# Moving the loads and stores of a second Strassen level to two other DMA queues, and two activations to later places

## The chip, the cores and the metric

The kernel runs on one core of one Trainium2 chip. A core has five engines with an instruction queue each: TensorE (PE: matrix products into the banks of PSUM, with its weight loads PEld beside them), VectorE (DVE), ScalarE (ACT), GpSimd (POOL) and SyncE (SP). [...] SyncE, ScalarE and GpSimd can issue DMA transfers, which 16 DMA engines carry out; the issue is an instruction in the queue of the engine that makes it, and what stands behind it in that queue comes after it. The metric is the device time of one execution in microseconds (us).

## What is computed

A layer: normalization, attention over the feature axis, residual; normalization, gated feed-forward, residual. Its weights gate, up and down are looked up by index in a table of 16 floats.

```python
def _L0_ffn_ref(x, lut, gate_idx, up_idx, down_idx):
    def _ghost_linear(x, idx, lut):
        w = lut[idx]
        return jnp.einsum('bsh,oh->bso', x, w)
    gate = _ghost_linear(x, gate_idx, lut)
    up = _ghost_linear(x, up_idx, lut)
    h = jax.nn.silu(gate) * up
    return _ghost_linear(h, down_idx, lut)
x = x + _L0_attn_ref(_layernorm(x, axis=-1), Wq, Wk, Wv, Wo)
x = x + _L0_ffn_ref(_layernorm(x, axis=-1), lut, gate_idx, up_idx, down_idx)
```

x is (2, 2048, 512) in fp32, so 4096 rows of 512 features; the inner width is 1376; all is fp32. The change lies in gate, up and their product h.

## The kernel before, in words

The 4096 rows are 8 chunks of 512, taken in 4 pairs p = 0 to 3. The inner width is 11 tiles f = 0 to 10, of 128 columns and a last one of 96. One **unit** (f, p) computes h for 128 inner columns and two chunks: h0 for chunk 2p, h1 for chunk 2p + 1. It takes gate and up together as one 2 x 2 block product and does it in Strassen's way (Winograd's form), with seven products instead of eight. A product of a unit is two matmuls of 128x128 by 128x512; each matmul shows as two records in the profile. Their sums pass through the banks a (two), b, c (two): product a1 goes into bank a, ScalarE copies it out to p1, a2 is added into the same bank, ScalarE copies u2, a3 is added, VectorE takes c22, a4 is added, and so on. **TensorE may add the next product into the bank only when the copy before has been made**: a2 waits for the copy p1 (L1058), a3 for the copy u2 (L1082).

For f = 2 to 9 there is a **second level**: some of a unit's products belong to a further 2 x 2 block product over two tiles f (even, odd) and two pairs p (even, odd), of which there are three, c, b and d (class Second, L888), with the banks z, x and w, one each. A unit then has a role: 0 is (even f, even p), 1 is (even, odd), 2 is (odd, even), 3 is (odd, odd); the tiles f = 0, 1 and 10 have none. The group of four units is spread over time, since all p of an even f come first, so parts of the sums have to be kept:

- Second.sums (L897): during units (1, 2) to (2, 0) VectorE makes the operand sums T1, T2, T4 for each of c, b, d and the two groups g of pairs, 18 tiles of 256 KB in four rotating buffers "rt". Each is stored to DRAM, far_c0T1 and so on (L908).
- Second.load (L917): loads() asks for them again ahead of a unit: six (T2 and T1 of the three) for the unit after a role-0 unit's start, that is ahead of (even f, even p) for (even f, odd p), and three (T4) ahead of (even f, last p) and (odd f, second p) for the role-2 unit that follows (L920).
- Second.part (L952): in role 1 six sums (r6 and r5 of c, d, b) are copied out of their banks by ScalarE into an "rt" buffer and stored to DRAM (L963); in role 2 r5 is added to by an accumulating DMA on GpSimd's queue (L958).
- Second.add_part (L965): in roles 2 and 3 a kept part of b is added to p1, one of c to v, by accumulating loads on GpSimd's queue (L968).
- Second.back (L970): in roles 2 and 3 a kept part of d is loaded into y (L973), which has one buffer. Role 2 adds w's product to y, and a4 adds y to bank a to give h1.

Line.run (L1190) writes the order out by hand: the steps of a unit u, with those of the unit before it, `last`, between them. Each call of between() puts work of VectorE into the gap: sums that are due, or a slice of the lookup of the next weights. The order is that of each engine's instructions, except on GpSimd, whose queue is ordered by a scheduler. In words, a unit is: a1 and the copy of bank a (p1); gap; for roles 1 to 3 of `last` the product h0 with u2 and h0's store; extra0 (z); c1 with the copies p7 and, in roles 2 and 3, v; gap; extra1; `last`'s a4 with the sum and silu of h1; a2 and the copy u2 (for role 3 a2 comes before `last`'s a4); gap; extra2; c2; `last`'s product of h1 with c22 and h1's store (end); gap; extra3; then b (h0's sum and silu) and a3 (c22), in this order for role 0, role 2 and units without a role, with a gap between and after.

The temporaries p1 (roles 1 to 3), p7, u2, v, y, c22, h0 and h1 have one buffer each, so the next unit's copy waits for the last reader. The index tiles of the lookup (two buffers) are loaded on GpSimd's queue (L311, L330, L359).

In the diff, file lines from L1146 on move by a few: L1156 of the kernel before (h0's product) is L1159 after, L1146 (h0's silu) is L1144 or, for role 1, L1149, L1178 (h1's silu) is L1184, L1181 (h1's product) is L1187, L1138 and L1165, L1170 (copies h0, h1) are L1135, L1168, L1173.

Of the kernel before, what the change touches and what calls it, by code (L numbers as in the profile page):

```python
# [55 lines left out]
AF = mybir.ActivationFunctionType  # L56
# [13 lines left out]
def tile_attn_ffn(  # L70
# [13 lines left out]
    nc = tc.nc  # L84
# [51 lines left out]
    def sub(dest, a, b):  # L136
        nc.vector.tensor_tensor(dest, a, b, ALU.subtract)

    def add(dest, a, b):
        nc.vector.tensor_tensor(dest, a, b, ALU.add)  # L140
# [337 lines left out]
    def left(t, name, order=("S2", "S4", "S1")):  # L478
        a11, a21 = t[:, 0:2, :H], t[:, 0:2, H:]
        a12, a22 = t[:, 2:4, :H], t[:, 2:4, H:]  # L480

        def s3():
            for tag in order:
                o.new(tag)
            sub(a21, a11, a21)
            o.update({"11": a11, "12": a12, "22": a22, "S3": a21})

        o = Operand(name, [
            s3, lambda: sub(o["S2"], a22, a21), lambda: sub(o["S4"], a12, o["S2"]),
            lambda: add(o["S1"], o["S2"], a11),  # L490
        ])
        return o
# [111 lines left out]
    class Square:  # L604
# [7 lines left out]
        def mm(self, ps, a, b, first):  # L612
            for m in range(2):
                for k in range(2):

                    nc.tensor.matmul(
                        ps[:, m, :], self.a[a][:, k, m * P : (m + 1) * P], self.b[b][:, k, :],
                        start=first and m == k == 0, stop=k == 1,
                        skip_group_check=not (first and m == 0),
                    )  # L620
# [50 lines left out]
    class Softmax:  # L671
# [20 lines left out]
        def end(self, h):  # L692
            r = slice(2 * h, 2 * h + 2)
            nc.vector.reciprocal(self.inv[:, r], self.sum[:, r])
            for m in range(2 * h, 2 * h + 2):
                nc.scalar.activation(
                    self.a[:, m, :], self.a[:, m, :], AF.Copy, scale=self.inv[:, m : m + 1]
                )

    gram_out(1)  # L700
    g = [g_ops[0], left(gs[1], "g_1")]
# [186 lines left out]
    class Second:  # L888
# [8 lines left out]
        def sums(self, g):  # L897

            (b11, b21), (b12, b22) = (self.operand(2 * g + h) for h in range(2))
            r = self.right[g] = {"11": b11, "21": b21, "22": b22, "T3": b12}  # L900

            def made(tag, u, v):
                r[tag] = x2p.tile([P, CH], F32, tag="rt", name=f"{tag}_{self.name}{g}", bufs=RT)
                sub(r[tag], u(), v())
                far = self.far[g, tag] = dram.tile(
                    [P, CH], F32, tag=f"{self.name}{g}{tag}", name=f"far_{self.name}{g}{tag}"
                )
                nc.sync.dma_start(far, r[tag])  # L908

            return [  # L910
                lambda: made("T1", lambda: b12, lambda: b11),
                lambda: made("T2", lambda: b22, lambda: r["T1"]),
                lambda: sub(b12, b22, b12),
                lambda: made("T4", lambda: b21, lambda: r["T2"]),
            ]

        def load(self, g, *tags):  # L917
            for tag in tags:
                t = x2p.tile([P, CH], F32, tag="tt", name=f"{tag}_{self.name}{g}_in", bufs=9)
                nc.sync.dma_start(t, self.far[g, tag])  # L920
                self.right[g][tag] = t

        def ready(self, f):
# [28 lines left out]
        def part(self, u, tag, onto=False):  # L952

            g = u.p // 2
            t = x2p.tile([P, CH], F32, tag="rt", name=f"{tag}_{self.name}_{u.name}", bufs=RT)
            nc.scalar.copy(t, self.ps)
            if onto:
                nc.gpsimd.dma_start(self.parts[g, tag], t, accum_op=ALU.add)  # L958
                return
            to = self.parts[g, tag] = dram.tile(  # L960
                [P, CH], F32, tag=f"{self.name}{g}{tag}", name=f"part_{tag}_{self.name}_{u.name}"
            )
            nc.sync.dma_start(to, t)  # L963

        def add_part(self, u, dest):  # L965
            tag = {2: "r6", 3: "r5"}.get(u.role)
# [3 lines left out]
        def back(self, u):  # L970

            t = u.temp("y")
            nc.sync.dma_start(t, self.parts[u.p // 2, {2: "r6", 3: "r5"}[u.role]])  # L973
            return t

    RT = 4
# [6 lines left out]
    of_d = Second("d", "w", lambda f: in_two(gu[f]["S4"]), lambda p: in_two(xs[p]["22"]))  # L983
# [42 lines left out]
    class GateUp:  # L1026
# [52 lines left out]
        def a2(self):  # L1079
            mm(self.a, self.pairs("S2", "T2"), False)  # L1080
            self.u2 = self.temp("u2")
            nc.scalar.copy(self.u2, self.a)  # L1082
            if self.role == 2:
                self.y = of_d.back(self)

        def c2(self):
            if self.role is None:
# [30 lines left out]
        def extra3(self):  # L1118
            if self.role == 1:
                of_d.go_on(self, "S1", "T1")  # L1120
                of_d.part(self, "r5")
                of_b.go_on(self, "S1", "T1")
                of_b.part(self, "r5")
            elif self.role == 2:
                of_d.begin(self, "S3", "T3")
                of_d.part(self, "r5", onto=True)
                add(self.y, of_d.ps, self.y)
            elif self.role == 3:
                self.y = of_d.back(self)

        def b(self):
            self.h0 = h0 = self.temp("h0")
            if self.role is None:
                mm(self.p1, self.pairs("12", "21"), False)
            elif self.role == 0:  # L1135
                of_b.begin(self, "11", "11")
                mm(self.p1, of_b.pair(self, "12", "21"), False)
                nc.scalar.copy(h0, of_b.ps)  # L1138
                add(h0, self.p1, h0)
            elif self.role == 1:  # L1140
                of_b.go_on(self, "S4", "22")
                add(h0, of_b.ps, self.p1)
            elif self.role == 2:
                of_b.go_on(self, "22", "T4")  # L1144
                add(h0, of_b.ps, self.p1)
            nc.scalar.activation(h0, self.p1 if self.role in (None, 3) else h0, AF.Silu)  # L1146

        def a3(self):
            mm(self.a, self.pairs("S1", "T1"), False)  # L1149
# [9 lines left out]
        def a4(self):  # L1159
            self.h1 = h1 = self.temp("h1")  # L1160
            if self.role is None:
                mm(self.a, self.pairs("S4", "22"), False)
            elif self.role == 0:
                of_d.begin(self, "11", "11")
                nc.scalar.copy(h1, of_d.ps)  # L1165
                mm(self.a, of_d.pair(self, "12", "21"), False)
                add(h1, self.a, h1)
            elif self.role == 1:  # L1168
                of_d.go_on(self, "S4", "22")
                nc.scalar.copy(h1, of_d.ps)  # L1170
                add(h1, self.a, h1)
            else:
                if self.role == 2:  # L1173
                    mm(self.a, of_d.pair(self, "22", "T4"), False)
                add(h1, self.a, self.y)
            if self.p == NPR - 1:
                ended[0] = self.f + 1
            nc.scalar.activation(h1, self.a if self.role is None else h1, AF.Silu)  # L1178

        def end(self):  # L1180
            nc.vector.tensor_tensor(self.h1, self.h1, self.c22, ALU.mult)  # L1181
            self.store(self.h1, 2 * self.p + 1)

    class Line:  # L1184
# [5 lines left out]
        def run(self, u, final=False):  # L1190
            last, self.last = self.last, u

            def last_a4():
                if last is not None:
                    last.a4()
                    self.between()

            role = getattr(u, "role", None)
            u.a1()
            self.between()  # L1200
            if getattr(last, "role", None):
                last.first()
            u.extra0()
            u.c1()
            self.between()
            u.extra1()
            if role != 3:
                last_a4()
            u.a2()
            self.between()  # L1210
            if role == 3:
                last_a4()
            u.extra2()
            u.c2()
            if last is not None:
                last.end()
            self.between()
            u.extra3()
            one, two = (u.a3, u.b) if final or role in (1, 3) else (u.b, u.a3)
            one()  # L1220
            self.between()
            two()
            if not role:
                u.first()
            self.between()

        def flush(self):
            self.last.a4()
            self.last.end()
            self.last = None  # L1230

    pace = [1.0]
# [94 lines left out]
    class Down:  # L1327
# [96 lines left out]
        def first(self):  # L1424
            pass

        extra0 = extra1 = extra2 = extra3 = first

        def end(self):
            pass  # L1430

    rows_in, normed_in = {}, []

# [22 lines left out]
    for (f, p), following in zip(units, units[1:] + [(NFT, 0)]):  # L1456
# [24 lines left out]
        u = GateUp(f, p)  # L1481
# [16 lines left out]
    for (part, c), following in zip(parts, parts[1:] + [None]):  # L1498
        nxt = None
        for jj in range(2):  # L1500
# [18 lines left out]
            u = units.pop(0)  # L1519
# [64 lines left out]
```

## Time and profile before

| | |
|---|---|
| median of 3 runs | 1088.44 us (1086.99 to 1089.98) |
| the profiled execution | 1091.63 us, of which its span 1089.8 us |
| TensorE busy | 1070.0 us, 98% of the span |
| VectorE busy | 838.6 us, 77% |
| ScalarE busy | 399.5 us, 37% |
| GpSimd busy | 85.7 us, 8% |
| granted TensorE clock, mean of the span | 0.994 |
| DMA moved | 189.06 MB, 173 GB/s |
| gate-and-up stage | from about 298 us to 818 us of the span |

Busy time counts instructions that compute; an engine that waits or issues a DMA is not busy. TensorE's busy time takes a matmul's modelled end, so 98% says that there is hardly a gap between matmuls, not that they run at their peak. The span is the time from the first to the last instruction; the rest of the execution's time lies around it. "a <- b" in a wait reads: a could start when b had ended. Names are without buffer numbers, so `h` is h0 or h1, `y<-part_r_d` is the load of y, `T_c_in<-far_c1T` one of Second.load's. In a row of the timeline the square brackets hold the engine's idle time before the instruction and what ended it.

### The profile page before, as it was taken

To read this page: it belongs to the slowest core of one execution; us is meant where nothing else is said; L and a number is where in the kernel's file an instruction comes from. 1 tells how busy PE (TensorE), PEld (TensorE's weight loads), DVE (VectorE), ACT (ScalarE), POOL (GpSimd) and SP (SyncE) were. 2 spreads that over 40 slices of the span, in tenths; PEclk is the share of its full clock that TensorE was granted. 3 is DMA by queue.
4 is the path that set the end of the run, shared out by engine and by line. 5 is a ranking of instruction groups with operands and counts; after the bars stand their busy time and mean duration, and the time that the engine had idled before them with its cause. 6 is when DMAs were issued, how large, how long until landed. Compare 5 with 4: busy or idle time off the path is not lost. (4 is left out here: it accounts for less than half of the span.)

```text
span 1089.8 us, 11426 instructions
## 1 busy us (share of the span) xinstructions
PE 1070.0 (98%) x3410; PEld 639.8 (59%) x3410; DVE 838.6 (77%) x1838; ACT 399.5 (37%) x759; POOL 85.7 (8%) x126
## 2 busy tenths in 40 slices
PE   9999999999999989999999998999999999999998
PEld 5668886444444434434444443444348888888887
DVE  7888777889885979789689988865629999555554
ACT  4652522554622224434444443444323322211111
POOL 0000000021110000220121022013000000000000
PEclk9999999999999989999999999999999999999999
DMA  8750314588651365785495588559526675656773
GB/s 345 224 164 20 77 40 97 138 231 217 172 140 39 144 203 202 187 184 205 147 223 175 193 198 186 190 171 199 146 73 217 203 236 173 209 177 222 226 227 117
DMA packets 127070, 189.06 MB, mean 173 GB/s; under 512 B 18576, under 2 KB 54672, under 8 KB 126112
## 3 DMA queue, kind: packets, MB, share of 16 engines
q1 hardware_dynamic: 93888, 140.55, 39.9%
q0 software_dynamic: 13056, 31.01, 14.7%
q10 hardware_dynamic: 20064, 16.78, 4.8%
q8 instruction: 27, 0.44, 0.2%
q14 instruction: 35, 0.29, 0.1%
HBM read 108.60 MB, written 79.69 MB: 173 GB/s over the span
## 5 line engine op out<-in xcount | busy, mean ns | idle before, releaser
L779 PE MATMUL y<-m,nT 128*128 128x512 f32 x256 | 110.2, 592 | 0.0
L1021 PE MATMUL c_g<-xb,wu 128*128 128x512 f32 (+1 forms) x176 | 84.4, 603 | 0.0
L779 PEld LDWEIGHTS y<-m,nT 128*128 128x128 f32 x256 | 48.6, 190 | 60.4 <-issue 57.4
L1021 PE MATMUL a_g<-xb,wg 128*128 128x512 f32 (+1 forms) x176 | 83.7, 598 | 0.0
L1021 PE MATMUL a_g<-xT_a,s 128*128 128x512 f32 (+1 forms) x176 | 83.2, 595 | 0.5 <-ACT p L1058 0.3
L1021 PE MATMUL a_d<-dT,hs_a 128*128 128x256 f32 x288 | 72.6, 379 | 0.0
L463 PE MATMUL gp<-xn_a 128*128 128x128 f32 (+3 forms) x256 | 70.1, 434 | 1.1 <-DVE xn_a L181 0.8
L1021 PE MATMUL a_g<-xT_sq,s 128*128 128x512 f32 (+1 forms) x132 | 63.2, 601 | 3.1 <-ACT u L1082 3.1
L463 PEld LDWEIGHTS gp<-xn_a 128*128 128x128 f32 x256 | 43.9, 190 | 28.0 <-issue 15.1
L1021 PEld LDWEIGHTS c_g<-xb,wu 128*128 128x128 f32 (+1 forms) x176 | 33.6, 191 | 43.6 <-issue 43.4
L1021 PEld LDWEIGHTS a_g<-xb,wg 128*128 128x128 f32 (+1 forms) x176 | 33.4, 190 | 43.9 <-issue 39.8
L1021 PEld LDWEIGHTS a_d<-dT,hs_a 128*128 128x128 f32 x288 | 54.5, 189 | 7.7
L1021 PEld LDWEIGHTS a_g<-xT_a,s 128*128 128x128 f32 (+1 forms) x176 | 32.6, 187 | 44.4 <-issue 39.2
L294 DVE COPY_PREDICATED wd<-b_wd,wd 128x512 f32<-128x512 int16 (+1 forms) x77 | 56.4, 732 | 1.3
L1387 ACT COPY p_d<-a_d 128x256 f32<-128x256 f32 x32 | 11.9, 372 | 120.8 <-PE a_d L1021 120.8
L140 DVE TENSOR_TENSOR r<-r,p_d 128x256 f32<-128x256 f32 x64 | 27.0, 421 | 27.0 <-ACT p_d L1387 17.0
L282 DVE TENSOR_SCALAR wd<-idx_wd,lut_x,lut_sb 128x512 int32<-128x512 int32 (+1 forms) x88 | 46.0, 538 | 0.7 <-DMA hd<-h 0.7
L1021 PEld LDWEIGHTS a_g<-xT_sq,s 128*128 128x128 f32 (+1 forms) x132 | 24.7, 189 | 36.4 <-issue 28.8
L140 DVE TENSOR_TENSOR u<-c_g,u 128x512 f32<-128x512 f32 (+1 forms) x28 | 19.3, 688 | 34.5 <-PE c_g L1021 31.9
L140 DVE TENSOR_TENSOR c<-a_g,p 128x512 f32<-128x512 f32 (+1 forms) x44 | 30.1, 685 | 17.5 <-PE a_g L1021 17.1
L140 DVE TENSOR_TENSOR r<-r,a_d 128x256 f32<-128x256 f32 x64 | 26.6, 416 | 22.0 <-PE a_d L1021 21.9
L1146 ACT ACTIVATE h<-h 128x512 f32<-128x512 f32 x24 | 15.1, 631 | 76.5 <-DVE h L140 69.5
(342 smaller groups left out, 2206.3 us busy)
## 6 DMA issues: line engine op xcount, KB each, us to landing
hd<-h SPq DMA_DIRECT2D x80, 256.0 KB, 2.2
h<-hd SPq DMA_DIRECT2D x40, 512.0 KB, 6.2
nl<-nd SPq DMA_DIRECT2D x32, 256.0 KB, 5.8
xnd<-xn_f ACTq DMA_DIRECT2D x16, 512.0 KB, 6.1
fl<-xnd POOLq DMA_DIRECT2D x32, 256.0 KB, 6.7
xn_back<-xnd SPq DMA_DIRECT2D x32, 256.0 KB, 4.4
rd<-r SPq DMA_DIRECT2D x32, 256.0 KB, 3.1
r<-rd SPq DMA_DIRECT2D x32, 256.0 KB, 3.6
```

The source lines that it names most:

```text
L140: nc.vector.tensor_tensor(dest, a, b, ALU.add)
L282: vec.tensor_scalar(dest.bitcast(I32), idx, lut_x[:rows, k : k + 1], lut_i[:rows, at : at + 1], ALU.bitwise_and, ALU.bitwise_xor,)
L294: vec.copy_predicated(dest, masks[level - 1], t)
L463: nc.tensor.matmul(gp[b][i][:, i * P :], xn[:, i, j % 2, :], xn[:, i:, j % 2, :], start=c % CPB == 0 and j == 0, stop=c % CPB == CPB - 1 a ...
L779: nc.tensor.matmul(ys[k], nTs[k][:, i, :], m[:, i, :], start=(i == 0), stop=(i == KB - 1))
L1021: nc.tensor.matmul(ps, lhsT, rhs, start=first and i == 0, stop=i == len(pairs) - 1, skip_group_check=not first,)
L1146: nc.scalar.activation(h0, self.p1 if self.role in (None, 3) else h0, AF.Silu)
L1387: nc.scalar.copy(p1, self.a)
```

## The change

It gives four kinds of DMA another queue, and moves four steps:

- Second.sums stores the operand sums from GpSimd's queue, not SyncE's (18 transfers of 256 KB).
- Second.load loads them on ScalarE's queue (72), and Second.part stores role 1's parts there (48).
- Second.back loads y on GpSimd's queue (16). In role 2 it is called in extra3, where it was called behind a2, and w's product is added to y in a4, one unit later, where it was added in extra3.
- Role 1's silu of h0 is called behind the next unit's a1, so behind its copy of bank a, where it stood at the end of b.
- The silu of h1 is called in end (behind c2), where it stood in a4; the product of h1 with c22 and the store move to a new step, out, behind extra3.

SyncE's queue keeps the stores of h0 and h1 in this stage. The products and sums themselves, and TensorE's order, stay.

```diff
@@ Second.sums
-                nc.sync.dma_start(far, r[tag])
+                nc.gpsimd.dma_start(far, r[tag])
@@ Second.load
-                nc.sync.dma_start(t, self.far[g, tag])
+                nc.scalar.dma_start(t, self.far[g, tag])
@@ Second.part
-            nc.sync.dma_start(to, t)
+            nc.scalar.dma_start(to, t)
@@ Second.back
-            nc.sync.dma_start(t, self.parts[u.p // 2, {2: "r6", 3: "r5"}[u.role]])
+            nc.gpsimd.dma_start(t, self.parts[u.p // 2, {2: "r6", 3: "r5"}[u.role]])
@@ GateUp.a2
             nc.scalar.copy(self.u2, self.a)
-            if self.role == 2:
-                self.y = of_d.back(self)
@@ GateUp.extra3
             elif self.role == 2:
                 of_d.begin(self, "S3", "T3")
                 of_d.part(self, "r5", onto=True)
-                add(self.y, of_d.ps, self.y)
-            elif self.role == 3:
+            if self.role in (2, 3):
                 self.y = of_d.back(self)
@@ GateUp.b
-            nc.scalar.activation(h0, self.p1 if self.role in (None, 3) else h0, AF.Silu)
+            if self.role != 1:
+                nc.scalar.activation(h0, self.p1 if self.role in (None, 3) else h0, AF.Silu)
+
+        def silu(self):
+
+            if self.role == 1:
+                nc.scalar.activation(self.h0, self.h0, AF.Silu)
@@ GateUp.a4
                 if self.role == 2:
                     mm(self.a, of_d.pair(self, "22", "T4"), False)
+                    add(self.y, of_d.ps, self.y)
                 add(h1, self.a, self.y)
             if self.p == NPR - 1:
                 ended[0] = self.f + 1
-            nc.scalar.activation(h1, self.a if self.role is None else h1, AF.Silu)
 
         def end(self):
+            nc.scalar.activation(self.h1, self.a if self.role is None else self.h1, AF.Silu)
+
+        def out(self):
             nc.vector.tensor_tensor(self.h1, self.h1, self.c22, ALU.mult)
             self.store(self.h1, 2 * self.p + 1)
@@ Line.run
             u.a1()
+            if last is not None:
+                last.silu()
             self.between()
...
             u.extra3()
+            if last is not None:
+                last.out()
             one, two = (u.a3, u.b) if final or role in (1, 3) else (u.b, u.a3)
@@ Line.flush
             self.last.end()
+            self.last.out()
```

Class Down, which the same line runs afterwards, gets the new steps as empty ones.

More of the change, by code (lines that the diff above doesn't have):

```diff
@@ L1425, in first @@
             pass
-        extra0 = extra1 = extra2 = extra3 = first
-        def end(self):
-            pass
+        extra0 = extra1 = extra2 = extra3 = silu = end = out = first
     rows_in, normed_in = {}, []
```

## The prediction

> **What bounds the kernel now.** I read the page first (TensorE busy 98% of the span), then TensorE's waits, which say where it stands still, and then the timeline around each of them. The waits (waiting instruction, who released it, total us, times, longest):
>
> ```profile
> PE z_g L1021 <- DVE lc L137: 5.3, 1, 5.3
> PE a_g L1021 <- ACT p L1058: 4.8, 4, 1.9
> PE a_g L1021 <- ACT u L1082: 3.1, 2, 1.9
> ```
>
> All of them fall into the gate-and-up stage, between 399 and 674 us. Elsewhere TensorE runs matmul behind matmul, 0.43 us a record (`PE a_g L1021 x8` takes 3.43 us in the chain), so the change can gain only what these stalls cost. The timeline (start, duration, what, idle before it and its releaser) shows the worst of the second and third kind, units (7,2) and (7,3):
>
> ```profile
> 659.01 0.68 DVE L140 TENSOR_TENSOR h<-a_g,y 128x512 f32<-128x512 f32 x1
> 659.72 0.32 SPq L973 DMA_DIRECT2D y<-part_r_d  x1
> ...
> 666.37 0.69 DVE L140 TENSOR_TENSOR y<-w_g,y 128x512 f32<-128x512 f32 x1 [2.59 <-DMA y<-part_r_d]
> 666.98 0.68 DVE L140 TENSOR_TENSOR h<-x_g,p 128x512 f32<-128x512 f32 x1
> ...
> 667.69 0.63 ACT L1146 ACTIVATE h<-h 128x512 f32<-128x512 f32 x1 [5.86 <-DVE h L140]
> ...
> 668.23 0.57 ACT L1058 COPY p<-a_g 128x512 f32<-128x512 f32 x1
> ...
> 668.85 1.98 PE L1021 MATMUL a_g<-xT_x,s 128*128 128x512 f32 x4 [1.75 <-ACT p L1058]
> ...
> 672.07 0.59 ACT L1076 COPY v<-c_g 128x512 f32<-128x512 f32 x1 [2.05 <-DVE u L140]
> ...
> 672.92 0.59 ACT L1082 COPY u<-a_g 128x512 f32<-128x512 f32 x1 [0.26 <-DVE h L1156]
> ...
> 673.56 2.86 PE L1021 MATMUL a_g<-xT_sq,s 128*128 128x512 f32 x4 [1.87 <-ACT u L1082]
> ```
>
> y has one buffer, so its load starts when the last y has been added (659.7) and lands 6.6 us later. VectorE needs it at once for y += w and stands 2.59 us. Behind that in its queue stands h0's sum, behind that ScalarE's silu, behind that in ScalarE's queue the copy of bank a (p), on which TensorE waits. The same delay comes again through v and u2. After a stall the clock is lower too (granted clock 0.83 in 670 to 680 us): the next eight records take 2.65 and 2.58 us a four instead of 1.72. The same happens at 476.65 (VectorE 2.69 us) and 570.67 (1.72 us).
>
> The first kind comes at the last operand sums of f = 1:
>
> ```profile
> 385.28 2.38 SPq L908 DMA_DIRECT2D far_c1T<-T_c  x3
> ...
> 392.77 0.69 DVE L137 TENSOR_TENSOR T_b<-xb,T_b 128x512 f32<-128x512 f32 x1 [5.86 <-DMA far_c1T<-T_c]
> ...
> 399.50 2.08 PE L1021 MATMUL z_g<-T_c_in,lc 128*128 128x512 f32 x2 [5.32 <-DVE lc L137]
> ```
>
> The store far_c1T1 stands on SyncE's queue behind six T loads (382.18 to 385.1 us) and lands after 7.4 us. Its "rt" buffer (4) is wanted again at 386.9, so VectorE stands 5.86 us and the sums lc come late.
>
> **What the stalls cost.** Start to start, against 0.43 us a record. First y place: c starts 475.39, the u2 product should start ten records later, at 479.69, and starts at 483.51: 3.8 us. Second: 577.26 instead of 574.67: 2.6. Third: 673.56 instead of 669.52, and 1.8 more on the slow clock: 5.8. Sum 12.2. The far stall: z at 399.50 instead of 394.03, then 5.29 us for the next six records instead of 2.58: 8.2.
>
> **y.** Loading y moves to GpSimd's queue (16 DMAs), role 2's add from the gap behind w's product to the next unit's a4, about ten program matmuls (8.6 us) later. The load still waits for the same buffer (h's add, 659.7), so it is not sooner. GpSimd is then in the store part_r_b (until 660.2). An accumulating load of that queue takes 0.87 us to issue and a median of 4.7 us to land (3.8 to 7.2), so y is there at 665 to 667.5, and is wanted at about 670: the stall is gone with 2 us to spare. Without that cover it would be late by what the landing exceeds. What is late next: VectorE gains the wait and 0.6 us of the add, so u2 += v comes 3.3, 2.3 and 3.2 us sooner at the three places. Followed through v's and u2's copies (0.59 us each) TensorE then waits 0.2, 0.4 and 1.0 us at the u2 product.
>
> **ScalarE's issues.** It gets 48 part stores and 72 T loads. It has issued such DMAs before only in the first stage, with four pieces to a row:
>
> ```profile
> 30.95 0.80 ACT L236 ACTIVATE n<-x,nmr_a,rstd_a 128x512 f32<-128x512 f32 x1
> 31.77 0.58 ACTq L562 DMA_DIRECT2D nd<-n  x1
> 32.40 0.81 ACT L236 ACTIVATE xn_a<-x,nmr_a,rstd_a 128x512 f32<-128x512 f32 x1 [0.66 <-ACT n L236]
> ...
> 488.16 0.38 SPq L920 DMA_DIRECT2D T_b_in<-far_b0T  x1
> ...
> 488.64 0.38 SPq L920 DMA_DIRECT2D T_d_in<-far_d0T  x1
> ```
>
> An issue there is 0.52 us; SyncE's same shape (xn_back) starts at 0.52, and its part stores and T loads are 0.32 to 0.41. I take the lower bound, since engine and shape agree: 0.5 us for a store with its gap, 0.47 for a load (488.16 to 488.64). Upper bound 1.1 us, the longest T loads on SyncE (1.09, 1.22).
> - Role 1, eight units: in the burst at 410 us the copies r_d, r_b, h1's silu (now here), a cast, r_d, r_b and their stores end at 414.93 instead of 414.2; the product on x wants it at 415.13. I take 0.15 us a unit: 1.2 us (0 to 2.8, with 0.52 for an issue).
> - Six loads ahead of the copy of bank a, 2.8 us. Into (f,2): loads end near 418.3, the copy was 418.11, TensorE wants it by 420.28: nothing. Into units (4,0), (6,0), (8,0): the silu of h0 waits for the store of the last h0 to land (675.93 at the third place) or for p's accumulation; 3.2 us sooner at the third, it ends at 672.6, loads to 675.4, copy to 676; TensorE wants it at 674.67, nine and a half us after a1. So 1.3, 1.1 and 1.5 us at the three places, the stalls above included: 3.9 (0 to 7.8, if p lands late). It takes the place of 12.2: gain 8.3.
> - Three loads into (f,1) and slow issues at a full DMA (1.22 us at 642.6): I take 1.0 us (0 to 3).
>
> **far by GpSimd's queue (18 stores), T loads by ScalarE's.** The loads can go after silu of h0 at 379.4, 2.8 us sooner, and the store no longer stands behind them. It is made at 383.76, lands after 4.7 to 7.2 us as GpSimd's others do: 388.5 to 391 instead of 392.77. VectorE gains 1.8 to 4.3 us; I take 3.0. TensorE then stands 2.5 us, and I leave 1.5 us for the slow clock: 4.2 us gained (0 to 7). In the earlier sums (362 us) VectorE may lose 1 to 2 us, hidden by its idle 1.49 us at 377.13.
>
> **The moved silus.** The same 0.63 us each; role 1's goes behind the copy of bank a, h1's behind u2's copy. ScalarE waits 34.8 us for h1's sum and 69.5 us for h0's, but only the stalls above reach TensorE: nothing beyond them. If the later store of h1 held the next h1 copy, ScalarE would stand; it has 6.9 us for product, store and landing (0.7 + 0.3 + 2.1).
>
> **Sum.** -8.3 - 4.2 + 1.2 + 1.0 = -10.3 us. The profiled execution (span 1089.8 us, 1091.6 with what lies around it) would come to a span of 1079.5; it ran 3.2 us above the median of three, 1088.44, so the median comes to 1078.1.
>
> **Rivals.** (1) ScalarE's queue becomes the bound, slower. At 1.1 us an issue a burst of six takes 6.6 us, 3.8 more: 3 x 3.8 into (4,0), (6,0), (8,0); 4 x 2.4 into (f,2), where 1.4 us is free; 1.5 into (2,0): 22.5 us, net +12.2, 1100.6 us. It decides from 0.85 us an issue. For it: SyncE's T loads did reach 0.83 to 1.22 when the DMA engines were full, and a blocked issue holds ScalarE's copies, not idle SyncE; so does an issue whose semaphore (the program shares eight among SyncE's and ScalarE's transfers) is still taken by a transfer under way. Against it: their median is 0.38 to 0.41.
> (2) The far store gains nothing: six loads of 256 KB before it move 1.6 MB whichever queue asks, and the engines' share is 0.8 to 1.0 in such stretches. Then -10.3 + 4.2: 1082.3 us. [...] The trace can't settle it: here one queue carried both.
> (3) VectorE's backlog keeps the stalls: it is busy 0.9 in 440 to 470 and 660 to 690, and the y add only moves. Only the 0.6 us of the add, through p and u2, is won at each place: 3.6; no far gain; 2.4 lost: 1087.2. Against it: the waits of 1.7 to 2.7 us are idle time, and the whole delay of silu follows them.
>
> **How the numbers follow.** Forecast 0.48, (1) 0.22, (2) 0.17, (3) 0.13. The likeliest's own range is 1072 to 1085, from the bounds of its terms; the range is 1070 to 1094, which leaves out most of the worst of (1). A change below 0.3% (3.3 us, 1085.2 to 1091.7) could not be told from none. Faster: forecast and (2), 0.65; same: (3), less what of it is faster, 0.12; slower: 0.23.
>
> **What would show it.** Right: no VectorE wait on y before h0's sum; TensorE's waits on p and u2 below 1.6 us each at 477, 572, 667; a wait on b (L1058) at the start of (4,0), (6,0), (8,0) of about 1 us, with six T loads on ScalarE's queue before it; VectorE's far wait at 387 below 4.1 us. Wrong: T loads on ScalarE's queue over 0.85 us apart, ScalarE behind TensorE at every (f,2), or VectorE standing as long on far as before.

## The result and the profile after

| | before | after |
|---|---|---|
| median | 1087.8 us (4 runs, 1086.99 to 1089.98) | 1078.45 us (4 runs, 1077.27 to 1080.96) |
| ratio, 95% interval | | 0.9914 (0.989 to 0.9938) |
| the profiled execution | 1091.63 us, span 1089.8 | 1077.27 us, span 1075.3 |
| TensorE's waits in the gate-and-up stage | 13.2 us | 5.8 us |
| mean granted clock | 0.994 | 1.000 |

The change saves 9.4 us by the medians, but 14.4 us between the two profiled executions: that of before lies at the upper end of what the kernel before took in later runs (most of them between 1085 and 1091 us), that of after is the shortest of its four. What follows from the two traces is the places, not the total.

TensorE's waits of the changed kernel in that stage (who waited, for whom, total us, times, longest), and after them the only wait of VectorE's there for a far store:

```profile
PE a_g L1021 <- ACT b_g L1058: 4.3, 3, 2.0
PE z_g L1021 <- DVE lc L137: 1.2, 1, 1.2
PE z_g L1021 <- ACT r_c L956: 0.3, 1, 0.3
```

```profile
DVE T_b L137 <- DMA far_c1T<-T_c: 1.8, 1, 1.8
```

The waits on p and u are gone, the wait on lc has shrunk from 5.3 to 1.2 us, and three waits for a copy of bank a are new. VectorE waits for y nowhere. The timeline at units (7,2) and (7,3), where the worst y stall of before lay:

```profile
648.67 1.15 POOL L973 DMA_DIRECT2D y<-part_r_d  x1
...
652.38 0.68 DVE L140 TENSOR_TENSOR h<-x_g,p 128x512 f32<-128x512 f32 x1
653.10 0.63 ACT L1144 ACTIVATE h<-h 128x512 f32<-128x512 f32 x1 [2.11 <-DVE h L140]
...
654.70 0.59 ACT L1058 COPY p<-a_g 128x512 f32<-128x512 f32 x1 [0.97 <-PE a_g L1021]
...
658.64 0.67 DVE L140 TENSOR_TENSOR y<-w_g,y 128x512 f32<-128x512 f32 x1
```

y is still asked for only when its buffer comes free, but its sum now stands behind h0's sum in VectorE's queue, ten microseconds after the load. So h0's sum, its silu and the copy p no longer wait for that DMA; ScalarE waits for TensorE (0.97 us), no longer TensorE for ScalarE.

The start of the same matmul in both profiles shows where the time went (lead: before minus after):

| matmul | before | after | lead, us |
|---|---|---|---|
| first on lc (z) | 399.50 | 395.67 | 3.83 |
| six records later | 404.79 | 398.35 | 6.44 |
| second z, unit (2,3) | 431.44 | 425.43 | 6.01 |
| behind (3,3)'s y stall | 483.51 | 473.69 | 9.82 |
| a2 of (4,0) | 488.66 | 479.92 | 8.74 |
| behind (5,3)'s y stall | 577.26 | 565.94 | 11.32 |
| a2 of (6,0) | 582.51 | 572.76 | 9.75 |
| behind (7,3)'s y stall | 678.79 | 662.36 | 16.43 |
| a2 of (8,0) | 680.51 | 666.24 | 14.27 |

Won: 6.4 us at f = 1, and 3.8, 2.6 and 6.7 us at the three y stalls (0.8 of the last already at 647 to 650 us, the rest at the stall itself). Lost: 0.4 us at (2,3), and 1.1, 1.6 and 2.2 us at the starts of (4,0), (6,0), (8,0). The last of these in the timeline of after:

```profile
662.70 0.63 ACT L1144 ACTIVATE h<-p 128x512 f32<-128x512 f32 x1 [1.94 <-DMA hd<-h]
662.73 0.83 ACTq L920 DMA_DIRECT2D T_c_in<-far_c0T  x2
663.59 0.54 ACTq L920 DMA_DIRECT2D T_d_in<-far_d0T  x1
664.16 0.45 ACTq L920 DMA_DIRECT2D T_b_in<-far_b0T  x1
664.64 0.45 ACTq L920 DMA_DIRECT2D T_d_in<-far_d0T  x1
665.13 0.45 ACTq L920 DMA_DIRECT2D T_b_in<-far_b0T  x1
665.62 0.57 ACT L1058 COPY b_g<-a_g 128x512 f32<-128x512 f32 x1 [2.29 <-DMA T_c_in<-far_c0T]
...
666.24 1.98 PE L1021 MATMUL a_g<-xT_sq,s 128*128 128x512 f32 x4 [2.00 <-ACT b_g L1058]
```

Six issues fill ScalarE's queue from 662.73 to 665.6; the copy that TensorE wants at 664.24 (2.00 us before its matmul starts) stands behind them.

### The profile page after: what moved, and what is told of

Read it like the earlier page. It is cut to its first block, busy times and chain, and to the rows that moved or that the text cites. A ratio compares the mean times of both kernels' runs of the same rounds, so it can differ in the third digit from the quotient of the medians.

```text
span 1075.3 us, 11377 instructions
## 1 busy us (share of the span) xinstructions
PE 1063.2 (99%) x3410; PEld 637.7 (59%) x3410; DVE 839.2 (78%) x1838; ACT 397.9 (37%) x759; POOL 104.3 (10%) x160
## 5 line engine op out<-in xcount | busy, mean ns | idle before, releaser
L1082 ACT COPY u<-a_g 128x512 f32<-128x512 f32 (+1 forms) x44 | 25.8, 586 | 66.6 <-PE a_g L1021 62.9
```

## The experiments

"Ratio" is always to runs of the kernel before on the same chip, with its 95% interval. "Half clock" is a stretch in which the profile shows a granted TensorE clock of 0.50; in this stage such a stretch lasted 3.4 or 6.8 us in the runs that had one (in the kernel before 6.8, 3.4 and 3.4 us, from 398.0, 480.0 and 674.5 us on), and half of its length is counted as its price.

### One part of the change at a time, on the kernel before

**The step of y alone.**

```diff
-            nc.sync.dma_start(t, self.parts[u.p // 2, ...
+            nc.gpsimd.dma_start(t, self.parts[u.p // 2, ...
@@ GateUp.a2, extra3
-            if self.role == 2:
-                self.y = of_d.back(self)
...
-                add(self.y, of_d.ps, self.y)
-            elif self.role == 3:
+            if self.role in (2, 3):
                 self.y = of_d.back(self)
@@ GateUp.a4
                     mm(self.a, of_d.pair(self, "22", "T4"), False)
+                    add(self.y, of_d.ps, self.y)
```

> The kernel before with the step of y alone (load of y by GpSimd's queue in extra3, w's product added in a4); loads, parts and silus stay. Forecast's theory: VectorE's three waits on y ahead of h0's sum (2.69, 1.72, 2.59 us) go, and with them 12 to 13 us of TensorE's lost time near 475, 570 and 670 us; since the T loads stay on SyncE's queue, nothing holds the copy of bank a into (4,0), (6,0), (8,0), so no more than 1.6 us comes back: 1087.8 - 11 = 1077 us, ratio about 0.990. Rival (VectorE's backlog keeps the stalls): only the 0.6 us of the add is won at each place, 3.6 us: 1084 us, ratio 0.997, and TensorE still waits over 1 us for p or u at the three places.

Measured: 1079.28 us, ratio 0.9922 (0.9909 to 0.9936). No wait of VectorE's on y ahead of h0's sum, and of TensorE's waits at the three places 0.3, 0.3 and 0.4 us for u are left, none for a copy into (4,0), (6,0), (8,0). VectorE's backlog as the cause (rival 3) is out.

**Of this step, the moved sum alone**: y stays on SyncE's queue, in its old place.

```diff
-                add(self.y, of_d.ps, self.y)
             elif self.role == 3:
@@ GateUp.a4
                     mm(self.a, of_d.pair(self, "22", "T4"), False)
+                    add(self.y, of_d.ps, self.y)
```

> The kernel before with w's product added to y in a4, one unit later, and nothing else: y's load stays on SyncE's queue where it was. Theory (the sum is made 8.6 us later, that is the whole of it): no wait on y at the three places, 1079.3 us as with the whole step of y, ratio 0.992. Rival (SyncE's queue, in which h stores and T loads stand behind the load that waits for its buffer, makes y late too): waits of 1 us or more on y or on T tiles remain, 1083 us or more, ratio 0.996.

Measured: 1078.24 us, ratio 0.9909 (0.9896 to 0.9922), the same as the whole change. Its waits, TensorE's and (last) VectorE's:

```profile
PE z_g L1021 <- DVE lc L137: 3.7, 1, 3.7
PE a_g L1021 <- ACT u L1082: 1.1, 3, 0.5
```

```profile
DVE T_b L137 <- DMA far_c1T<-T_c: 4.2, 1, 4.2
```

The far stall is still there, as nothing at f = 1 was changed; the y stalls are gone. GpSimd's queue is not needed for them.

**The far stores alone, and the T loads alone.**

```diff
-                nc.sync.dma_start(far, r[tag])
+                nc.gpsimd.dma_start(far, r[tag])
```

> The kernel before with the far stores by GpSimd's queue alone; the T loads stay on SyncE's. Theory A (the store's place behind six loads on one queue was the delay): far_c1T1 is issued near 383.8 us and lands in about 3 us as in the changed kernel, VectorE's far wait falls from 5.86 to about 1.8 us, the gain is the changed kernel's whole 6 us: ratio 0.9945. Theory B (the transfers share the DMA engines, and the loads asked for from 382.2 us on are ahead of the store whichever queue asks): the store lands at 389 us or later, the wait stays above 4 us, the gain is under 2 us: ratio 0.998 or more.

```diff
-                nc.sync.dma_start(t, self.far[g, tag])
+                nc.scalar.dma_start(t, self.far[g, tag])
```

> The kernel before with the T loads by ScalarE's queue alone; the far stores stay on SyncE's. At f = 1: the six loads go at 379 us, 3 us sooner, and the store stands behind nothing. Theory A and theory B (see the run of the far stores) both expect VectorE's far wait near 2 us and some 6 us gained here; if the wait stays above 4 us here and falls in the other run, GpSimd's queue itself is what helps. Later: the six loads stand ahead of the copy of bank a into (4,0), (6,0), (8,0), where the y stalls of the kernel before are still there: 2.5 to 3 us each on top, as silu of h0 is no sooner, some 5 to 9 us lost. Net: between -1 and +3 us, ratio 0.999 to 1.003. Rival: the copy has that much room, the net is -6 us, 0.9945.

Measured: far stores 1083.87 us, ratio 0.9963 (0.995 to 0.9977); T loads 1094.89 us, ratio 1.0069 (1.0054 to 1.0084). At f = 1 the two timelines read, far stores alone first:

```profile
382.63 0.90 SPq L920 DMA_DIRECT2D T_c_in<-far_c0T  x2
...
384.47 0.54 POOL L908 DMA_DIRECT2D far_c1T<-T_c  x1 [2.69 <-DVE T_c L137]
...
391.56 0.69 DVE L137 TENSOR_TENSOR T_b<-xb,T_b 128x512 f32<-128x512 f32 x1 [4.23 <-DMA far_c1T<-T_c]
```

and T loads alone:

```profile
378.71 1.05 ACTq L920 DMA_DIRECT2D T_c_in<-far_c0T  x2
...
383.67 2.25 SPq L908 DMA_DIRECT2D far_c1T<-T_c  x3
...
387.69 0.69 DVE L137 TENSOR_TENSOR T_b<-xb,T_b 128x512 f32<-128x512 f32 x1 [0.90 <-DMA far_c1T<-T_c]
```

With a queue of its own the store is issued at 384.47 us and has landed at 391.5, hardly sooner or later than on SyncE's queue behind the loads in the kernels with the y step or the moved sum alone (VectorE goes on at 391.4 and 390.9; both wait 4.2 us too). With the loads 4 us sooner it lands at 387.6 from SyncE's own queue. So it is the loads' transfers that delay it, whichever queue asks: theory B. Why the far stores alone still give 3.7 us in the median, where theory B allowed under 2, is not shown: their profile has smaller y stalls (VectorE waits 6.3 us on y in all) and a shorter stretch of half clock at 398 us than the kernel before, but no link from the edit to these is shown.

The T loads alone lose 7.3 us by the medians (the profiled execution is the shortest of its six): at the starts of (f,2) and of two units (f,0) TensorE waits 0.5 to 1.8 us for the copy of bank a behind them (6.8 us in all), on top of the y stalls. The expectation had put this loss at the (f,0) alone.

### One part of the change taken back, on the changed kernel

**The step of y undone** (the first diff backwards).

> The changed kernel with the whole step of y undone (load on SyncE's queue behind a2, w's product added in role 2's own gap); all other edits stay. If the moved add is the whole net gain and the rest of the change cancels out (the T loads sooner at f = 1 against their burst ahead of the copy of bank a), the y stalls come back in full: VectorE waits 1.7 to 3 us on y at three places, the time is that of the kernel before, 1085 to 1091 us, ratio 0.997 to 1.003. If the other edits gain the 5 us of f = 1 net, 1082 to 1084 us, ratio 0.995; the sum of the forecast without its y term expects 1086 us.

Measured: 1087.45 us, ratio 0.9993 (0.9979 to 1.0006). VectorE waits on y again:

```profile
DVE y L140 <- DMA y<-part_r_d: 8.5, 5, 2.6
```

By the medians all the other edits together are worth nothing. The other side shows the same: the moved sum alone took 1078.24 us, the whole change 1078.45.

**The far stores back on SyncE's queue.**

```diff
-                nc.gpsimd.dma_start(far, r[tag])
+                nc.sync.dma_start(far, r[tag])
```

> The changed kernel with the far stores back on SyncE's queue; the T loads stay on ScalarE's. Theory B (what counts is when the six loads are asked for, 379 us instead of 382, and not whose queue the store stands in): VectorE's far wait stays between 1 and 2.5 us, TensorE's wait for lc between 0 and 2 us, the time is the changed kernel's, 1078.4 us, ratio to the kernel before 0.9914. Theory A (the store needs a queue of its own): the wait goes back above 4 us, 4 to 6 us slower, ratio 0.996.

Measured: 1079.25 us, ratio 0.992 (0.9904 to 0.9935), VectorE's far wait 2.1 us, TensorE's for lc 1.6: theory B again.

**Role 1's silu of h0 back at the end of b.**

```diff
-            if self.role != 1:
+            if True:
                 nc.scalar.activation(h0, self.p1 if self.role in (None, 3) else h0, AF.Silu)
@@ GateUp.silu
-            if self.role == 1:
-                nc.scalar.activation(self.h0, self.h0, AF.Silu)
+            pass
```

> The changed kernel with role 1's silu of h0 back at the end of b, ahead of the T loads and of the next unit's copy of bank a. The forecast's step (the moved silus are worth nothing beyond the stalls): 1078.4 us, ratio 0.9914. Rival (the move is what lets the six T loads be issued before that copy is wanted): silu waits for h0's late sum, the loads start behind it, and TensorE waits 1.5 to 1.9 us for the copy at the start of the four units (2,2), (4,2), (6,2), (8,2): 6 to 7 us more, 1085 us, ratio 0.9975.

Measured: 1085.97 us, ratio 0.998 (0.9964 to 0.9997). TensorE's waits for that copy, and unit (2,2) in the timeline:

```profile
PE a_g L1021 <- ACT b_g L1058: 10.2, 7, 2.4
```

```profile
412.29 0.63 ACT L1144 ACTIVATE h<-h 128x512 f32<-128x512 f32 x1 [4.40 <-DVE h L140]
412.30 0.81 ACTq L920 DMA_DIRECT2D T_c_in<-far_c1T  x2
...
415.21 0.57 ACT L1058 COPY b_g<-a_g 128x512 f32<-128x512 f32 x1 [2.29 <-issue]
```

The loads stand behind a silu that has waited 4.40 us for h0's sum, and the copy behind the loads. In the changed kernel the silu stands behind the copy, and that burst begins at 408.8 us. Four waits of 2.37, 1.48, 0.55 and 0.87 us, at the starts of the four (f,2), are new, and one stretch of half clock: by the medians the move of the silu is worth 7.5 us, once the loads are on that queue.

**Twice as many issues**: each T load as two transfers of 64 partitions.

```diff
-                nc.scalar.dma_start(t, self.far[g, tag])
+                for q in range(2):
+                    at = slice(q * P // 2, (q + 1) * P // 2)
+                    nc.scalar.dma_start(t[at], self.far[g, tag][at])
```

> The changed kernel with each T load on ScalarE's queue issued as two transfers of 64 partitions, so that a burst is twelve issues and a load costs about 0.94 us of the queue, past the 0.85 us from which rival (1) was to decide. Rival (1)'s working at this price: the copy of bank a into (4,0), (6,0), (8,0) comes 2.8 us later than in the changed kernel, so TensorE's waits there grow from 0.83, 1.42, 2.00 to 3.6, 4.2, 4.8 us; into (2,2), (4,2), (6,2), (8,2) new waits of about 1.4 us or more each; with two or three stretches of half clock (1.7 us each) in all 14 to 20 us more, 1093 to 1098 us, ratio 1.005 to 1.01. Against it: the time that counts is the transfers', not the issues' (the copies wait no longer): 1078.4 us, 0.9914.

Measured: 1128.69 us, ratio 1.0369 (1.0355 to 1.0384): 50 us over the changed kernel, where 14 to 20 were expected. The burst into (4,0) in the timeline, and the clock of the span:

```profile
486.13 2.40 ACTq L922 DMA_DIRECT2D T_c_in<-far_c0T  x4
488.56 1.27 ACTq L922 DMA_DIRECT2D T_d_in<-far_d0T  x2
...
493.77 0.57 ACT L1060 COPY b_g<-a_g 128x512 f32<-128x512 f32 x1 [7.04 <-DMA T_b_in<-far_b0T]
```

```profile
core 0: 1126.4 us, clock 0.982
```

(The lines of this kernel lie two further down.) A half took mostly 0.61 us to issue where a whole load took 0.33 to 0.5, so a burst of six loads takes 7.6 us, not 5.6. TensorE waits 37.1 us for copies of bank a, 2.45 to 6.2 at each of the eight bursts of six, and a clock of 0.982 over 1126 us is some 20 us more. That ScalarE's queue decides is right; the price had the issues too cheap, and two or three stretches of half clock where there were seven, five of them of 6.8 us.

### The kernel before once more

> The kernel before, once more, for how far its stalls vary. The profile shown of it is the longest of its executions (1091.63 us; 16 others have a median of 1087.6). If the y stalls are what the program makes, VectorE's waits on y of 1.7 to 2.7 us stand at the same three places and TensorE loses 10 to 13 us there, and the difference lies in the far stall (its wait was 4.2 us in another kernel with the same code up to there) and in the stretches of half clock. If they are chance, one of the three places is free in this profile.

Measured: 1087.63 us, ratio 1.0001. The y stalls stand at the same three places (VectorE 9.0 us on y in all), TensorE's wait for lc is 3.9 us where it was 5.3, and there is one stretch of half clock less. So what was predicted from were stalls that the program makes, in an execution in which they cost some 3 us more than in this one.

### Better than both

**The T loads behind the next unit's copy of bank a**, in the changed kernel:

```diff
-        loads(*following)
         u = GateUp(f, p)
...
-        line.run(u, final=(f, p) == (NFT - 1, NPR - 1))
+        line.run(u, final=(f, p) == (NFT - 1, NPR - 1), ask=lambda: loads(*following))
@@ Line.run
             u.a1()
+            if ask is not None:
+                ask()
```

> The changed kernel with the T loads asked for behind the next unit's copy of bank a instead of ahead of it, on ScalarE's queue as before. Forecast's theory: TensorE's waits on that copy at the start of (4,0), (6,0), (8,0) (0.83, 1.42, 2.00 us) are the loads' six issues of 0.47 us; behind the copy they hold only p7's copy, which TensorE wants some 5 us later: 4 us less, 1074.3 us, ratio to the kernel before 0.9875. Rival: the late silu of h0 (it waits for the store of the last h0 to land) is what makes the copy late, the loads add nothing of their own: no change, 1078.4 us, 0.9914. Second rival: the loads land too late for the unit after, or p7's copy is late: waits on z, w, x or on p7, slower than 1078.4 us.

Measured: 1075.99 us, ratio 0.9892 (0.9876 to 0.9908). The three waits at (4,0), (6,0), (8,0) are gone. But at f = 1 the loads now go at 382.1 us again, and TensorE's only wait in the stage and VectorE's for the far store are:

```profile
PE z_g L1021 <- DVE lc L137: 3.1, 1, 3.1
DVE T_b L137 <- DMA far_c1T<-T_c: 3.6, 1, 3.6
```

Part of the gain is given back. Here loads and stores have a queue each as in the changed kernel, and the later loads alone bring the far stall back: theory B once more.

**Besides, the first six loads in unit (1,3)**, 12 us sooner:

```diff
+        asked = {(1, 3): (2, 1), (2, 0): (0, 0)}.get((f, p), following)
...
-        line.run(..., ask=lambda: loads(*following))
+        line.run(..., ask=lambda: loads(*asked))
```

> The kernel with the loads behind the copy of bank a, and besides it the first six T loads (for (2,1)) asked for in unit (1,3) instead of (2,0), some 11 us sooner, when the next far stores are not yet due. Theory B (what delays far_c1T1 is that the six loads' 1.5 MB is under way when it is stored): VectorE's far wait goes below 1 us, TensorE's wait for lc (3.07 us) and its stretch of half clock (1.7 us) go: 1075.99 - 4.5 = 1071.5 us, ratio 0.985. Rival (the store is delayed by other traffic of that time, as the index load at 380.6 us and the stores of h): the wait stays above 2 us, 1075 us, 0.989.

Measured: 1071.38 us, ratio 0.9838 (0.9824 to 0.9851), the best of all. TensorE's waits in the stage:

```profile
PE z_g L1021 <- DVE lc L137: 1.0, 1, 1.0
PE a_g L1021 <- ACT u L1082: 0.6, 1, 0.6
```

The time is as expected, though VectorE still waits 1.6 us for the far store, more than theory B allowed; the store it waits for takes 4.3 us to land, with nothing of the six loads under way, and what delays it is open.

**The moved sum and the first six loads sooner, on the kernel before, every queue as it was:**

```diff
+        loads(*{(2, 0): (0, 0)}.get((f, p), following))
-        loads(*following)
@@ Line.run
             u.a1()
+            if getattr(u, "name", "") == "1_3":
+                loads(2, 1)
```

(and the diff of the moved sum). 

> The kernel before with two edits alone, no queue changed: w's product added to y in a4 (one unit later), and the first six T loads asked for in unit (1,3) instead of (2,0). If all that the change brings comes from these two causes, it needs no other queue: of the kernel with the moved add alone (1078.24 us) TensorE's 3.68 us for lc and 1.7 us of half clock at 398 us go: 1073 us, ratio 0.9865, faster than the changed kernel. Rival: SyncE's queue, in which the six loads now wait for the far stores of the group before and h stores stand behind them, makes new waits: 1077 us or more.

Measured: 1073.37 us, ratio 0.9858 (0.9845 to 0.9871): better than the change without its queues. VectorE does not wait for a far store at all; the store lands in 2.0 us. The six loads go as early as in the run before (370.7 and 370.2 us), yet there the same store took 4.3 us from GpSimd's queue: once the loads are out of the way, the queue of its own was no help and may have cost 2 us (the two kernels differ in other queues too, so that is not shown).

## Why the prediction came out, point by point

- **What bounds it.** Right: nearly all that was won lies at the stalls named, at f = 1 and at three y places; elsewhere the lead hardly changes (0.8 us at 647 to 650 us).
- **y, 8.3 us.** Right in mechanism and size. In the two profiles the y stalls gave 3.81 + 2.58 + 6.68 = 13.1 us where 12.2 were put down, and the loads ahead of the copy took 1.08 + 1.57 + 2.16 = 4.8 back where 3.9 were. The waits on the copy were to be 1.3, 1.1 and 1.5 us and were 0.83, 1.42 and 2.00. The waits on u were taken for 0.2, 0.4 and 1.0 us; in the changed kernel there is none (with the moved sum alone 0.3 to 0.5). The step did not separate its two halves: the moved sum alone does it, and GpSimd's queue adds nothing.
- **far, 4.2 us.** The size was too small for the profile and the cause half wrong. The two profiles show 6.4 us: VectorE's wait fell by 4.1 us, where 3.0 were taken, and the whole stretch of half clock went. Against the runs with the moved sum or the y step alone, which stand at f = 1 as the kernel before does, it is 4.1 and 5.4 us, counted from the start of the stage. "The store no longer stands behind them" was given as one of two causes; it is none. Rival (2) had this part right: from its own queue the store landed no sooner, at 391.5 us. But the rival's result did not follow, since the loads were also asked for 3 us sooner, and that is the gain. How the DMA engines divide their time between the queues no run shows; the landings are what was measured.
- **Role 1's bursts, 1.2 us; T4 loads and slow issues, 1.0 us.** Too dear: one wait of 0.3 us, and none.
- **The moved silus, nothing.** Here a step failed, though the sum did not show it. The forecast put the loads into (f,2) at nothing, from times at which no late silu stands ahead of them, and put the silu's move at nothing on its own. The move is the cover of the other: without it the six loads start behind the late silu and cost 7.5 us. An edit that was priced at nothing by itself (it was not run alone) was half of another.
- **Rival (1).** Its threshold of 0.85 us was passed in five of 56 places only: ScalarE's loads mostly lay 0.36 to 0.57 us apart (the longest issue took 1.41). The run in halves shows that beyond it the loss is far greater than the 22.5 us that the rival put on 1.1 us an issue: at 1.27 us a load it was 50, since all eight bursts then reach TensorE and each of the seven waits of 3 us and more comes with half clock.
- **Rival (3).** Out: with the moved sum alone VectorE has the same work, and the y stalls are gone. In its sum, the 2.4 us lost are 2.2 by the forecast's own terms (1.2 + 1.0).
- **Sum.** -10.3 us was forecast for the profiled execution and its span fell by 14.5 us, but the medians differ by 9.4. The profiled execution of before was 4 us above the median of 16 later ones. Its stalls were the right places; as sizes they were high, and the forecast of 1078.1 us came close to 1078.45 because it subtracted the distance to the median, and because far was taken too small. That the number came within 0.4 us is therefore luck; the places and the size of the y term are not. The bounds of its terms, added up, give 1069 to 1090 us, wider than the 1072 to 1085 that it called its own range.

The whole: the moved sum alone is worth 9.7 us. Beside it the rest of the change wins some 4 to 5.5 us at f = 1, through the time at which six loads are asked for, and loses about as much again where six such loads stand ahead of a copy.

## What to carry to other kernels

Ask which engine's queue stands behind a wait for a DMA: moving the one instruction that waits behind the work that others need was worth as much here as the whole change (9.7 and 9.4 us), with no transfer moved. Where a DMA goes to a computing engine's queue, look at the urgent copy in that queue, and at what stands ahead of the DMA: six issues ahead of the copy of bank a made TensorE wait 0.83, 1.42 and 2.00 us at three places, and with a silu ahead of them that itself waited 4.40 us the time was 7.5 us longer. Before a transfer gets a queue of its own, look at what the DMA engines carry when it is issued: here a queue of its own left VectorE's wait for the far store at 4.2 us, and with the six other transfers asked for 11 us sooner and no queue changed there was none.

## What the runs showed of the hardware

- **Half clock came in stretches of 3.4 or 6.8 us.** In the kernel before, around the second stall (windows in us from the start; PE busy, then the other engines, granted clock, DMA share, GB/s):

```profile
476.50:480.00 3.50, 1.64 (x4) 0.49 (x3) 3.31 (x6) 1.26 (x3) 1.20 (x2) 0.99 0.33 63
480.00:483.40 3.40, 3.40 (x5) 1.17 (x4) 2.37 (x4) 1.61 (x3) 1.02 (x2) 0.50 0.80 151
483.40:486.80 3.40, 3.40 (x9) 1.60 (x9) 2.27 (x4) 1.15 (x2) 0.10 (x1) 1.00 0.84 167
```

  A stall of 1.86 us is followed by 3.4 us at 0.50, into which five records fall instead of nine. The three stretches of the kernel before start at 398.0 us, within the stall of 5.32 us, and at 480.0 and 674.5 us, 0.8 and 1.0 us after the starts of the matmuls that had waited 1.86 and 1.87 us. Half clock did not follow every stall: 1.86, 1.87, 2.05, 2.12 and 2.37 us brought it, 1.75, 2.00, 2.33 and 2.45 us did not, and every stall of 3.0 us or more in these runs did; what decides it is not shown. The price of a stall of some 2 us thus differs by 1.7 us, half of such a stretch, between these runs.
- **Half a transfer took longer to issue than a whole one**: mostly 0.61 us for 64 partitions (0.45 at the least), mostly 0.33 to 0.5 for 128, on ScalarE's queue. Why is not shown.
